# Issuing a 64-column matmul as two of 32 columns in the second half of a sparse graph layer

## The chip, the cores and the metric

The kernel runs on one core of a Trainium2 chip. The metric is the device time of one execution in microseconds. TensorE (PE in the profile) multiplies, with its weight loads counted apart (PEld); VectorE is DVE, ScalarE is ACT, GpSimd is POOL and SyncE is SP.

## What is computed

A graph layer over 4096 nodes, with eight batches of 256 features, all in float32. `x` has the shape (8, 4096, 256), `adj` (4096, 4096), `W` (256, 256).

```python
HW     = einsum('bnf,fo->bno', x, W)
A_norm = relu((adj + adj.T) * 0.5)
D      = sum(A_norm, axis=1)
d      = where(D > 0, where(D > 0, D, 1.0) ** -0.5, 0.0)
L      = eye(N) - d[:, None] * A_norm * d[None, :]
out    = relu(einsum('nm,bmo->bno', L, HW))
y      = layernorm(x + out)
```

The adjacency is sparse and falls off with the node number: the early nodes (hubs) have many neighbours, the late ones few.

## The kernel before

**First phase (to about 595 us).** The adjacency is read in blocks of 512 by 512, transposed on TensorE, added to its mirror, clipped and written to a DRAM tensor `a_dram`. Beside it the products of `x` and `W` are formed, scaled by the inverse root of the degree and written to `g_dram` (4096 rows of 2048 values: eight batches of 256). The block of output rows 0 (tile `lead`) is accumulated here as well.

**Second phase.** The other 31 blocks of 128 output rows are taken two at a time, as 16 units `u`, in the order of `SEQ`: 1 to 7, then 0, then 8 to 15. For a unit the kernel does not multiply by the whole adjacency. It packs the source nodes that have an edge to the unit into tiles of 128 nodes. Nodes are sorted by a kind, a number of four bits that says which of the four half blocks (two blocks, `b` = 0 and 1, with a lower and an upper half of 64 rows each) need them. `CAPS` fixes how many tiles of each kind a unit has; the lists of nodes are worked out on the chip, some units ahead (`patterns`, `place`, `place_rest`, `spread`, `collect`, `index`; their small bf16 matmuls are the lines L226 to L356).

For each tile GpSimd issues two indirect DMAs in `gather`: `ga`, the 128 rows of adjacency (L814, stationary operand), and `g`, the 128 rows of `g_dram` (L827, moving operand, 1 MB, in a ring of `RING` = 12 buffers). A further tile, `g_hub`, holds the first 128 nodes and stays in SBUF for the units in `HUB`.

The products are at L1032. An accumulator `py` of one block is four PSUM banks of 128 x 512 float32, one for each chunk `c` of the 2048 columns. Where a tile serves all 128 rows of a block, the product has 128 stationary columns. Where it serves one half block, it has 64 and writes partitions 0 to 63 or 64 to 127 of the bank. `steps_of` pairs tiles so that a lower and an upper half stand side by side in a step (kinds 1 with 2, 4 with 8, 5 with 10; kinds 6 and 9 hold both halves themselves), and the loop turns a step round where it would begin with the half in which the last one ended:

```python
if work[0][1] == side != slice(0, P):
    work.reverse()
```

Within a step the products of one chunk `c` follow each other, first over the entries of `work` and then over the chunks. Every issue on an engine is chained behind the one before it on that engine (`queue`), so the program's order is the code's order. When a block has had all its products, `finish` evicts its four banks on ScalarE (`evict`, L683), adds the residual and normalises on VectorE, and writes the result by a DMA of SyncE. `lists` puts the list work of later units between the steps of TensorE.

Of the kernel before, what the change touches and what calls it, by code (L numbers as in the profile page):

```python
# [59 lines left out]
def kernel(  # L60
# [25 lines left out]
    nc = tc.nc  # L86
    B, N, F = x.shape
    FO = w.shape[1]
    P = 128
    S = 512  # L90
# [6 lines left out]
    Q = 64  # L97
# [77 lines left out]
    def blocks(u):  # L175

        return min(2, NB - 1 - 2 * u)
# [561 lines left out]
    def targets(u, kind):  # L739

        if kind == 0:
            kind = 15 if blocks(u) == 2 else 3
        out = []
        for b in range(2):
            h = kind >> 2 * b & 3
            if h:
                out.append((b, {1: slice(0, Q), 2: slice(Q, P), 3: slice(0, P)}[h]))
        return out
# [19 lines left out]
    with (  # L768
# [23 lines left out]
        def queue(engine):  # L792

            traced = reversed(nc.cur_bb.bb.instructions)
            return tc.issue_after(next(i for i in traced if i.engine == engines[engine]))

        def gather(n):

            if n >= len(order):
                return  # L800
            u, kind, t = order[n]
            both = len(targets(u, kind)) == 2
            at = apool.tile([P, 2 * P], F32, tag="a", name=f"ga_{u}_{t % tmax}")
            if t < 0:
                if not hub_loads:
                    with queue("pool"):
                        hub_loads.append(nc.gpsimd.dma_start(hub, g_dram[:P, :]))
                with queue("pool"):
                    nc.gpsimd.dma_start(at, a_dram[:P, (2 * u + 1) * P : (2 * u + 3) * P])
                got[u, t] = (at, hub)  # L810
                return
            gi, ai = plan[u]
            with queue("pool"):
                nc.gpsimd.indirect_dma_start(  # L814
                    out=at if both else at[:, :P],
                    out_offset=None,
                    in_=a_pairs if both else a_rows,
                    in_offset=bass.IndirectOffsetOnAxis(ap=ai[:, t : t + 1], axis=0),
                    element_offset=P if both else 0,
                )  # L820


            n = len(ring_tiles)
            gt = ring[n % RING]
            ring_tiles.append(gt)
            with queue("pool"):
                nc.gpsimd.indirect_dma_start(  # L827
                    out=gt,
                    out_offset=None,
                    in_=g_dram,  # L830
                    in_offset=bass.IndirectOffsetOnAxis(ap=gi[:, t : t + 1], axis=0),
                    bounds_check=N if n < RING else N - 1,
                    oob_is_err=False,
                )
            got[u, t] = (at, gt)
# [4 lines left out]
        def after(n, fn, *args):  # L840
            later.append((n, fn, args))

        def run_later(by):
            ready = [l for l in later if l[0] <= by]
            later[:] = [(n - by, fn, args) for n, fn, args in later if n > by]
            for _, fn, args in ready:
                fn(*args)


        u = SEQ[0]  # L850
# [4 lines left out]
        py = {0: lead}  # L855
        left = {}
# [50 lines left out]
        def finish(i):  # L907

            if i == NB - 1:
                finish_last(i)  # L910
                return
            with queue("act"):
                y = evict(i, py.pop(i), ypool)

            def rest():
                z = xr.pop(i)
                with queue("dve"):
                    mv, var = moments(i, y, z, stat)
                with queue("dve"):
                    rstd = inverse_root(i, var, stat)  # L920

                def end():
                    in_turn(normalise, i, z, mv, rstd)

                after(3, end)

            after(1, rest)
# [66 lines left out]
        for q, (u, step) in enumerate(steps):  # L994
            new = q == 0 or steps[q - 1][0] != u
            last = q + 1 == len(steps) or steps[q + 1][0] != u
            if new:
                after(6, prepare, u)
                if q > 0:
                    after(10 if u != SEQ[-1] else 4, residuals, range(2 * u + 1, 2 * u + 1 + blocks(u)))  # L1000
                left = {}
                for v, st in steps[q:]:
                    if v == u:
                        for k, t in st:
                            for b, _ in targets(u, k):
                                left[b] = left.get(b, 0) + 1
                begun = set()
                for b in range(blocks(u)):
                    py[2 * u + 1 + b] = []
            work = [(b, rows, *got[u, t]) for m in range(2) for k, t in step for b, rows in targets(u, k)[m : m + 1]]  # L1010
            if work[0][1] == side != slice(0, P):
                work.reverse()
            side = work[-1][1]
            for b in sorted({wk[0] for wk in work}):
                if not py[2 * u + 1 + b]:
                    py[2 * u + 1 + b] = [
                        psum.tile([P, S], F32, tag=f"b{b}", name=f"py_{u}_{b}_{c}") for c in range(G // S)
                    ]
            fresh = []
            for b, rows, at, gt in work:  # L1020
                hs = {(b, h) for h in range(2) if rows.start <= h * Q < rows.stop}
                assert not hs & begun or hs <= begun
                fresh.append(not hs & begun)
                begun |= hs
                left[b] -= 1
            for c in range(G // S):
                for (b, rows, at, gt), new_rows in zip(work, fresh):
                    both = any(len(targets(u, k)) == 2 for k, t in step)
                    off = b * P if both else 0

                    with queue("pe"):
                        nc.tensor.matmul(  # L1032
                            py[2 * u + 1 + b][c][rows, :],
                            lhsT=at[:, off + rows.start : off + rows.stop],
                            rhs=gt[:, c * S : (c + 1) * S],
                            start=new_rows,
                            stop=left[b] == 0,
                            skip_group_check=True,
                        )
            for k, t in step:  # L1040
                gather(n)
                n += 1
            run_later(sum(1 + (rows == slice(0, P)) for _, rows, _, _ in work))
            for b in {wk[0] for wk in work}:
                if left[b] == 0:
                    finish(2 * u + 1 + b)
                    if b == 0:
                        after(2, lists, u)
# [9 lines left out]
    with tc.If(short > 0):  # L1058
        with (
# [4 lines left out]
            for i in range(NB):  # L1064
# [4 lines left out]
                py = [psum.tile([P, S], F32, tag="b0", name=f"pz_{i}_{c}") for c in range(G // S)]  # L1069
                for m in range(NB):  # L1070
                    gt = full.tile([P, G], F32, tag="g", name=f"gf_{i}_{m}", bufs=4)
                    nc.sync.dma_start(gt, g_dram[m * P : (m + 1) * P, :])
                    for c in range(G // S):
                        nc.tensor.matmul(
                            py[c],
                            lhsT=lt[:, m, :],
                            rhs=gt[:, c * S : (c + 1) * S],
                            start=(m == 0),
                            stop=(m == NB - 1),
# [33 lines left out]
```

## Time and profile before

| what | value |
|---|---|
| three runs | 1523.82, 1530.25, 1533.23 us (median 1530.25) |
| profiled execution | span 1527.5 us; a time of its own beside the span is not recorded |
| TensorE | 1441.2 us busy, 94% of the span, 6440 matmuls |
| weight loads | 763.6 us, 50% |
| VectorE | 983.6 us, 64% |
| GpSimd | 682.0 us, 45% |
| DMA | 564.50 MB, mean 370 GB/s |
| L1032, 64 columns | 2152 records, 494.7 us busy |
| L1032, 128 columns | 720 records with `g`, 176 with `g_hub`: 322.0 and 77.3 us busy |

The span is the time from the first to the last instruction of one execution. A row of a group reads: line, engine, operation, output and inputs, stationary shape, moving shape, count, then the busy time in us and the mean of one in ns, then the engine's idle time before it and what ended that. Busy time of a group counts overlapping records once, so busy time over count is the price of one where several run side by side, and the mean is how long one of them lasts. A row of the timeline reads: start and length in us, engine, line, operation, count. Ends of matmuls are modelled.

### The profile page before, as it was taken

What the parts mean: (1) busy time and instruction counts of PE and PEld (TensorE: products, weight loads), DVE (VectorE), ACT (ScalarE), POOL (GpSimd) and SP (SyncE); (2) the same over time, 40 slices, a digit from 0 to 9 for tenths busy, and PEclk for the clock granted to TensorE, in tenths of its full rate; (3) what the DMA queues carried; (4) which work ended last, traced back from release to release, by engine and by line L of the source; (5) the groups of instructions that cost most, each with busy time, mean ns of one, the idle gap of its engine ahead of it and who ended that gap; (6) DMA issues with size and microseconds to landing.
All of it is one profiled execution on the core that took longest, in us unless ns stands there. A gap on an engine that the chain in (4) does not pass through costs nothing.

```text
span 1527.5 us, 19332 instructions
## 1 busy us (share of the span) xinstructions
PE 1441.2 (94%) x6440; PEld 763.6 (50%) x6440; DVE 983.6 (64%) x3015; ACT 369.0 (24%) x462; POOL 682.0 (45%) x1051
## 2 busy tenths in 40 slices
PE   5999999989989989999999999999999999999995
PEld 5778777767767754433343343333433433333331
DVE  4676578888646463055568769569137688898534
ACT  3655554535434450010100100100010010001111
POOL 3002010010303316666667666666556676656653
PEclk9999999989999999999999999999999999999998
DMA  9999999999879898999999999999979999999995
GB/s 340 365 366 401 393 379 365 359 369 354 344 248 367 332 390 354 401 395 418 361 393 372 402 409 365 393 403 389 384 278 406 346 394 403 405 393 366 379 405 195
DMA packets 216714, 564.50 MB, mean 370 GB/s; under 512 B 16550, under 2 KB 104918, under 8 KB 180134
## 3 DMA queue, kind: packets, MB, share of 16 engines
q0 software_dynamic: 54224, 304.94, 50.4%
q1 hardware_dynamic: 93472, 126.89, 23.8%
q10 hardware_dynamic: 68912, 131.37, 22.7%
q8 instruction: 54, 0.88, 0.2%
q14 instruction: 52, 0.43, 0.1%
HBM read 443.61 MB, written 136.34 MB: 380 GB/s over the span
## 4 chain that ended last, share of the span: by engine, by line
PE 68%; DMA 14%; DVE 9%; issue 5%; POOL 2%; ACT 2%; ACTq 0%; DVEq 0%; POOLq 0%
PE py L1032 49%; PE pg L532 8%; DMA g<-g_dram,gi 6%; PE lead L490 5%; DMA a_dram<-sym 5%; DVE sym L427 3%; PE xtr L521 2%; PE tr L423 2%; DVE part L432 2%; DMA xin<-in_x_dram 2%; DMA ga<-a_dram,ai 1%; ACT sym L431 1%; PE lists L356 1%; ACT xt L522 1%; POOL g L827 0%
## 5 line engine op out<-in xcount | busy, mean ns | idle before, releaser
L1032 PE MATMUL py<-g,ga 128*64 128x512 f32 (+1 forms) x2872 | 813.0, 600 | 18.4 <-DMA g<-g_dram,gi 8.0
L1032 PEld LDWEIGHTS py<-g,ga 128*64 128x64 f32 (+1 forms) x2872 | 293.1, 151 | 525.1 <-issue 493.1
L827 POOL DMA_INDIRECT g<-g_dram,gi x268 | 294.9, 1101 | 219.1 <-PE py L1032 79.1
L814 POOL DMA_INDIRECT ga<-a_dram,ai x268 | 292.0, 1090 | 109.5 <-issue 76.8
L683 ACT ACTIVATE y<-py,minus_r 128x512 f32<-128x512 f32 x120 | 79.9, 687 | 812.3 <-PE py L1032 659.8
L693 DVE TENSOR_TENSOR xr<-xr,y 128x2048 f32<-128x2048 f32 x31 | 71.1, 2294 | 269.1 <-ACT y L683 267.2
L532 PE MATMUL pg<-w_sb,xt 128*128 128x256 f32 x1024 | 232.0, 385 | 5.2 <-ACT xt L522 5.2
L427 DVE TENSOR_TENSOR sym<-tr,adj 128x512 f32<-128x512 f32 x256 | 162.7, 683 | 96.9 <-PE tr L423 80.2
L532 PEld LDWEIGHTS pg<-w_sb,xt 128*128 128x128 f32 x1024 | 195.6, 194 | 33.4 <-ACT xt L522 5.6
L432 DVE TENSOR_REDUCE part<-sym 128x32 f32<-128x2048 f32 x64 | 145.5, 2279 | 62.0 <-ACT sym L431 62.0
L423 PE MATMUL tr<-ident,adj 128*128 128x128 f32 x1024 | 138.4, 285 | 30.6 <-DVE sym L427 19.2
L431 ACT ACTIVATE sym<-sym 128x2048 f32<-128x2048 f32 x64 | 122.6, 1916 | 129.9 <-DVE sym L427 117.5
L452 POOL TENSOR_TENSOR r<-e,neg_half 128x4 f32<-128x4 f32 x8 | 8.3, 1039 | 317.9 <-DVE e L451 236.5
L423 PEld LDWEIGHTS tr<-ident,adj 128*128 128x128 f32 x1024 | 118.6, 146 | 60.4 <-DVE sym L427 32.1
L521 PE MATMUL xtr<-ident,xin 128*128 128x128 f32 x512 | 72.4, 288 | 18.0 <-DVE sym L427 16.5
L702 DVE BATCH_NORM_STATS2 stats<-xr 128x6 f32<-128x256 f32 x256 | 87.0, 413 | 1.1
L726 DVE TENSOR_SCALAR xr<-xr,mv,root 128x256 f32<-128x256 f32 x248 | 83.6, 409 | 0.1
L490 PE MATMUL lead<-gt,strip 128*128 128x512 f32 x176 | 83.0, 598 | 0.0
L522 ACT COPY xt<-xtr 128x512 f32<-128x512 f32 x128 | 68.1, 591 | 46.7 <-PE xtr L521 46.0
L542 ACT ACTIVATE gt<-pg,r 128x512 f32<-128x512 f32 x88 | 60.6, 688 | 74.8 <-PE pg L532 72.3
L1032 PE MATMUL py<-g_hub,ga 128*128 128x512 f32 x176 | 77.3, 592 | 0.0
L521 PEld LDWEIGHTS xtr<-ident,xin 128*128 128x128 f32 x512 | 59.0, 146 | 34.9 <-DVE sym L427 26.4
(142 smaller groups left out, 825.8 us busy)
## 6 DMA issues: line engine op xcount, KB each, us to landing
adj<-in_adj_dram SPq DMA_DIRECT2D x64, 1024.0 KB
a_dram<-sym ACTq DMA_DIRECT2D x64, 1024.0 KB
out_dram<-xr SPq DMA_DIRECT2D x31, 1024.0 KB
xr<-in_x_dram ACTq DMA_DIRECT2D x29, 1024.0 KB
xin<-in_x_dram SPq DMA_DIRECT2D x44, 512.0 KB
g_dram<-gt ACTq DMA_DIRECT2D x22, 1024.0 KB
xin<-in_x_dram POOLq DMA_DIRECT2D x20, 512.0 KB
g_dram<-held ACTq DMA_DIRECT2D x10, 1024.0 KB
```

Of the source, the lines that this page charges most:

```text
L423: ins = nc.tensor.transpose(pt[:, c * P : (c + 1) * P], tji[:, c, a * P : (a + 1) * P], ident)
L427: nc.vector.tensor_add(sym[:, a, :], pt, tij[:, a, :])
L431: nc.scalar.activation(sym, sym, AF.Relu, scale=0.5)
L432: nc.vector.tensor_reduce(part[:, i * A : (i + 1) * A, j * S // Q : (j + 1) * S // Q], sym.rearrange("p a (c q) -> p a c q", q=Q), AX.X, A ...
L490: nc.tensor.matmul(lead[c], lhsT=strip, rhs=g[:, c * S : (c + 1) * S], start=not done, stop=len(done) == NB - 1, skip_group_check=True,)
L521: nc.tensor.transpose(pt[:, k, c, :], xin[b // H][:, b % H + k, c * P : (c + 1) * P], ident)
L532: ins = nc.tensor.matmul(pg[:, k * FO : (k + 1) * FO], lhsT=xt[:, b + k, c, :], rhs=w_sb[:, c, :], start=(c == 0), stop=(c == FC - 1),)
L702: nc.vector.bn_stats(stats[:, b, :], z[:, b, :])
L726: nc.vector.tensor_scalar(z[:, b, :], z[:, b, :], mv[:, b, 0:1], rstd[:, b : b + 1], ALU.subtract, ALU.mult,)
L814: nc.gpsimd.indirect_dma_start(out=at if both else at[:, :P], out_offset=None, in_=a_pairs if both else a_rows, in_offset=bass.IndirectOff ...
L827: nc.gpsimd.indirect_dma_start(out=gt, out_offset=None, in_=g_dram, in_offset=bass.IndirectOffsetOnAxis(ap=gi[:, t : t + 1], axis=0), boun ...
L1032: nc.tensor.matmul(py[2 * u + 1 + b][c][rows, :], lhsT=at[:, off + rows.start : off + rows.stop], rhs=gt[:, c * S : (c + 1) * S], start=ne ...
```

## The change

In units 8 to 15 a product with 64 stationary columns is issued as two products with 32 columns, over the same moving operand and into the same bank, each to its own 32 partitions. With a lower and an upper half in turn, successive products stand in the column places 0, 1, 2 and 3 of the array. Products of 128 columns, and all of units 0 to 7, stay as they are. The number of multiplications, the bytes moved and the order of the tiles do not change; the number of matmuls and weight loads does.

```diff
-                    with queue("pe"):
-                        nc.tensor.matmul(
-                            py[2 * u + 1 + b][c][rows, :],
-                            lhsT=at[:, off + rows.start : off + rows.stop],
-                            rhs=gt[:, c * S : (c + 1) * S],
-                            start=new_rows,
-                            stop=left[b] == 0,
-                            skip_group_check=True,
-                        )
+                    n_rows = rows.stop - rows.start
+                    by = P // 4 if n_rows == Q and u >= 8 else n_rows
+                    for lo in range(rows.start, rows.stop, by):
+                        with queue("pe"):
+                            nc.tensor.matmul(
+                                py[2 * u + 1 + b][c][lo : lo + by, :],
+                                lhsT=at[:, off + lo : off + lo + by],
+                                rhs=gt[:, c * S : (c + 1) * S],
+                                start=new_rows,
+                                stop=left[b] == 0,
+                                skip_group_check=True,
+                            )
```

## The prediction

> **What bounds the kernel now.** I read the page first (shares of the engines, slices over the span), then the chain of waits for the stretch of the units that change, then the groups by line with shapes kept apart, and last the weight loads in order of time. On the page:
>
> ```profile
> PE 1441.2 (94%) x6440; PEld 763.6 (50%) x6440; DVE 983.6 (64%) x3015; ACT 369.0 (24%) x462; POOL 682.0 (45%) x1051
> ...
> PE   5999999989989989999999999999999999999995
> ...
> DMA  9999999999879898999999999999979999999995
> ```
>
> TensorE (PE) is busy in nearly every slice, and so are the DMA engines: two resources stand close together. By counting the records of L1032 along the order that the program writes out, unit 8 begins at 1145.4 us and unit 15 ends at 1514.4 us, so the changed units fill 369.0 us. The chain of waits cut to that stretch says:
>
> ```profile
> by line: PE py L1032 62.9%; DMA g<-g_dram,gi 22.2%; DMA ga<-a_dram,ai 5.3%; issue 5.0%; POOL g L827 1.7%; POOL ga L814 0.8%; PE lists L356 0.7%; DVE xr L876 0.3%; DVE incl_k L184 0.2%; ACT y L866 0.2%; DVE pos_k L188 0.1%; PE lists L226 0.1
> ```
>
> The product sets the end for 62.9% of the stretch; the gathers of g and ga for 27.5% (the late units 13 to 15). So time added to L1032 goes to the end almost whole; time taken off it would soon meet the gathers. The groups over the whole span, shapes apart:
>
> ```profile
> L1032 PE MATMUL py<-g,ga 128*64 128x512 f32 x2152 | 494.7, 601 | 14.9 <-DMA g<-g_dram,gi 8.0 <-issue 3.8 <-DVE pos_k L188 2.2
> L1032 PE MATMUL py<-g,ga 128*128 128x512 f32 x720 | 322.0, 597 | 3.5 <-issue 3.0
> ...
> L1032 PEld LDWEIGHTS py<-g,ga 128*64 128x64 f32 x2152 | 159.4, 138 | 336.5 <-issue 314.8 <-DMA ga<-a_dram,ai 7.9 <-DMA g<-g_dram,gi 4.8
> L1032 PEld LDWEIGHTS py<-g,ga 128*128 128x128 f32 x720 | 133.7, 190 | 188.7 <-issue 178.3 <-DMA ga<-a_dram,ai 7.8 <-DMA g<-g_dram,gi 1.6
> ```
>
> Two things are to be seen. First, the counts: the code issues 1524 products in this loop, and the page has 2872 + 176 = 3048 records, so each float32 product is two records (a load and a matmul each, called a and b below). Second, one record of 128 columns takes 322.0/720 = 0.447 us of PE, one of 64 columns 494.7/2152 = 0.230 us, though each lasts about 600 ns alone. Two records of 64 columns therefore run side by side for the price of one wide one: half the array is not idle now. The loads in order of time, around the last step of unit 1 (a lone product in the lower half, four times) and the start of unit 2:
>
> ```profile
> 673.85 0.14 PEld L1032 LDWEIGHTS py<-g,ga 128*64 128x64 f32 x1 [0.29 <-issue]
> 674.28 0.14 PEld L1032 LDWEIGHTS py<-g,ga 128*64 128x64 f32 x1 [0.29 <-issue]
> 674.71 0.19 PEld L1032 LDWEIGHTS py<-g,ga 128*64 128x64 f32 x3 [0.29 <-issue]
> 675.14 0.14 PEld L1032 LDWEIGHTS py<-g,ga 128*64 128x64 f32 x1 [0.23 <-issue]
> ...
> 802.01 0.14 PEld L1032 LDWEIGHTS py<-g,ga 128*64 128x64 f32 x2 [0.28 <-issue]
> 802.44 0.14 PEld L1032 LDWEIGHTS py<-g,ga 128*64 128x64 f32 x2 [0.29 <-issue]
> 802.87 0.14 PEld L1032 LDWEIGHTS py<-g,ga 128*64 128x64 f32 x2 [0.29 <-issue]
> ```
>
> In the steady state (the last three lines) two loads come every 0.43 us; call 0.429 us a slot. In the first four lines one place works alone, one load a slot, and at 674.71 the other place joins while the lone product still has three records to run. It starts ahead of records that stand before it in the program.
>
> **What the Trainium skill says.** (1) "TensorEngine Tiling (Array Packing)", Key Properties: tiles load and multiply independently, and a change of tiling mode drains the array. The trace agrees for two columns (0.230 against 0.447 us), and from one form to the other the starts stand 0.522 us apart where 0.429 is usual, so a drain costs 0.093 us. (2) "TensorE: Matmul & The Clock Gate", Measured speedup vs the span model: three column tiles of 32 gave 2.38x, sixteen tiles of 32 by 32 gave 10.6x. No run here shows 32 columns, so this is my only support for four at once. (3) The same page, What overlaps and what doesn't: matmuls keep strict program order. The lines at 674.71 disagree, and I follow the trace. (4) "FP8 and Floating Point Precision", TensorE Precision Notes: true float32 takes four passes. That fits two records a product, each of 429 ns.
>
> **The change part by part.**
>
> *Slots.* Units 8 to 15 hold 114 half-width products for each of the four column chunks, 456 in all, hence 912 records of 64 columns. At two a slot they take 456 slots: 456 x 0.429 = 195.6 us. After the change there are 1824 records of 32 columns. At four a slot they take 1824/4 = 456 slots, again 195.6 us. A matmul streams the same 512 elements however few columns are loaded, so narrow ones pay only by standing side by side. Steps in which one half stands alone (in units 8 and 14) do not gain: their two pieces fill two of four places, in as many slots as now.
>
> *Order.* The program writes a and b of one place before the next place. In strict order only two neighbours could overlap. The trace showed a record starting past three pending ones; a piece of the fourth place must pass the b records of the other three, just that many. So four at once needs no more than has been seen, but no margin is shown.
>
> *Weight loads.* 912 more. From 138 ns at 64 columns and 190 at 128 I estimate 112 ns at 32 (0.81 ns a column). Each place needs one a slot, and loads of different places now run together (two in 0.14 us above), so 0.429 us covers them. Were they serial, four would take 0.45 us a slot: 456 x 0.02 = 9 us.
>
> *Issue.* 32 small products of the lists take 0.80 us in the chain (line L356), 25 ns for a load and a matmul. Four pairs need 0.10 us of a 0.429 us slot: hidden.
>
> *Changes of form.* The 64-column records of these units lie in 15 stretches between wide or bf16 work, and they stay 15, so their drains remain. If the fourth place trails by one slot, each stretch ends up to 0.43 us later: 0 to 6.4 us, and I take 0.5, since the order seen needs no trailing. New is the border from unit 0 (64 columns) to unit 8 (32): the upper half now starts three slots early beside the lone product there (at 1144.56, as at 674.71); behind a drain that is lost: 3 x 0.429 + 0.1 = 1.4 us.
>
> *What is untouched.* The gathers, the evictions (they wait for the last piece of a bank, up to 21 ns later at 7 ns a start), the bytes and every other engine's order. The ring of 12 is given back at the same slot.
>
> Sum: 0 + 0 + 0.5 + 1.4, about +2 us, with bounds 0 and +17 (6.4 + 9 + 1.4). A gain below nothing is excluded in the steady state because a slot is set by streaming; only jitter of gathers could give one. Against the profiled execution (span 1527.5 us; its own run among the three is not marked) this is 1529.5. The median of the runs, 1530.25, lies 2.75 above the span, so the same +2 gives about 1532.
>
> **The rivals.**
>
> *A, four at once (forecast):* 1532, own range 1524 to 1544.
>
> *B, partly side by side.* Four streams of float32 from SBUF, or four open places, are more than the trace has shown. With three places on average: 1824/3 = 608 slots, 152 more, 65 us. Waits for gathers inside the stretches give some back: the last stretches last 30.1, 14.0 and 13.4 us where slots ask 20.6, 10.3 and 12.0, so some 15 us can hide it. +50 us: 1580. For it: 64 columns show no sign of how many streams fit. Against it: two streams run without a nanosecond lost (429 in both forms).
>
> *C, two at once; this is the case on the other side.* If the array lets only two matmuls overlap, or keeps a and b in order so that only neighbours meet, each group of eight records takes four slots and not two: 912 slots, +195.6 us, less the 15: about 1711. For it: point (3), strict order. Against it: 674.71 and 1144.56. It decides as soon as a slot of four lasts over 0.429 + (15.3 + 15)/456 = 0.495 us, which is where the time leaves 1%.
>
> *D, faster.* Shorter loads in front of 15 stretches save 15 x 0.03 us; more could come only from gathers that happen to land better: 1526 at best likely.
>
> A change that does nothing would show 128*64 in units 8 to 15; the slices in the diff leave no room for that.
>
> **How the numbers follow.** A 0.59, B 0.17, C 0.20, D 0.04. A measurement of this kernel tells about 1% from no change. A lies within 1%; D mostly does too, with 0.02 beyond; B and C are slower, and I leave 0.03 of A's tail there. Hence faster 0.02, same 0.60, slower 0.38. The time is A's, 1532. To hold eight in ten the range takes in A, D and most of B, up to 1640, and leaves out C.
>
> **What would show it.** Right: a group 128*32 of 1824 records with 0.11 to 0.12 us of PE each, four loads together every 0.43 us, unit 8 to 15 in about 371 us, and the gathers still 20% to 30% of the chain there. Wrong: 0.15 us or more a record (B) or 0.21 to 0.23 (C), loads two by two at 0.43 us, gathers gone from the chain, and the waits of POOL for PE grown.

## The result

The change took 1548.41 us against 1528.66 for the kernel before (medians of 4 each): ratio 1.0135, 95% interval 1.0114 to 1.0157. It is slower by about 20 us. The forecast was 1532, within 1% of no change; the measured time lies inside the range given and outside the forecast's own case (1524 to 1544).

The profiled execution spans 1543.6 us, 16.1 more than the one before. Lines of its page, the slices and the group that is new, with its loads:

```profile
PE 1461.4 (95%) x7352; PEld 779.0 (50%) x7352; DVE 983.3 (64%) x3015; ACT 369.5 (24%) x462; POOL 691.4 (45%) x1051
...
PE   5999989898979989999999999999999999999996
...
DMA  9999999999879998999999999999989999999995
```

```profile
L1035 PE MATMUL py<-g,ga 128*32 128x512 f32 x1824 | 226.5, 593 | 9.0 <-issue 7.1
...
L1035 PEld LDWEIGHTS py<-g,ga 128*32 128x32 f32 x1824 | 79.2, 110 | 149.8 <-issue 145.6
```

The 1824 records of 32 columns are there, and one costs 226.5/1824 = 0.124 us of PE. Two at a time would be 0.21. So four do run side by side, nearly always; the price at four without a gap is 0.429/4 = 0.107. The idle time before them is ended by "issue", not by a gather: TensorE waited for nothing that the profile shows. The chain of waits, cut from the start of unit 8 to the end of unit 15, says the same:

```profile
by line: PE py L1035 95.8%; issue 2.3%; PE lists L356 1.2%; DVE xr L876 0.3%; PE lists L226 0.2%; ACT y L866 0.2%; PE lists L227 0.2%; PE lists L303 0.0%; PE lists L302 0.0%
```

The gathers, 27.5% of this stretch before, are gone from it: TensorE became later than they are.

Where the time went is seen when the narrow records are cut into stretches between wide or bf16 work. A middle stretch (kinds 6, 9, 5 and 10) follows wide products. An edge stretch (kinds 4 and 8, then 1 and 2 of the next unit) follows the list products. Lengths in us, from the start of the first record to the start of what comes next; "slots" is the count of slots by 0.429:

| stretch | slots | before | change | change, other session (`change3` below) |
|---|---|---|---|---|
| middle of unit 9 | 13.73 | 13.88 | 13.87 | 13.87 |
| edge 8 to 9 | 13.73 | 13.88 | 19.82 | 13.87 |
| edge 9 to 10 | 13.73 | 14.35 | 19.87 | 13.87 |
| edge 10 to 11 | 13.73 | 13.88 | 19.81 | 13.87 |
| edge 11 to 12 | 10.30 | 14.54 | 15.11 | 14.38 |
| edge 12 to 13 | 13.73 | 13.88 | 17.02 | 13.87 |
| edge 13 to 14 | 12.01 | 13.88 | 17.57 | 13.87 |
| edge 14 to 15, no lists | 20.59 | 30.63 | 22.99 | 30.55 |

The seven edge rows come to 115.0 us before and 132.2 with the change, 17.2 more; the short stretch at the start of unit 8 adds 2.4. That makes 19.6 us, the loss of the medians. (In these two profiles the units ahead of unit 8 ended 2.7 us earlier with the change, so the spans differ by less.) The edge stretches alone would cost more, but the last one gives 7.6 us back: before, TensorE waited there for gathers, and a later TensorE does not. The loads in order of time, in the stretch from unit 9 to 10:

```profile
1258.15 0.11 PEld L1035 LDWEIGHTS py<-g,ga 128*32 128x32 f32 x1 [0.17 <-issue]
1258.58 0.19 PEld L1035 LDWEIGHTS py<-g,ga 128*32 128x32 f32 x2 [0.32 <-issue]
1259.39 0.11 PEld L1035 LDWEIGHTS py<-g,ga 128*32 128x32 f32 x1 [0.62 <-issue]
1260.79 0.14 PEld L1035 LDWEIGHTS py<-g,ga 128*32 128x32 f32 x2 [1.29 <-issue]
1262.21 0.14 PEld L1035 LDWEIGHTS py<-g,ga 128*32 128x32 f32 x2 [1.29 <-issue]
1263.64 0.24 PEld L1035 LDWEIGHTS py<-g,ga 128*32 128x32 f32 x8 [1.29 <-issue]
```

For 5 us only one or two loads come every 0.7 or 1.4 us, and at 1263.64 eight at once; such a place is called a thin spot below. The waits in front of these loads are all ended by "issue", none by a transfer. In the stretches at 13.87 us, four loads come every 0.43 us. The clock is not the reason: the mean granted clock is 0.984 in this profile and 0.981 in the one before.

### The profile page after: what moved, and what is told of

Same layout as the page of the kernel before. It is cut to its first block, busy times and chain, and to the rows that moved or that the text cites. A ratio compares the mean times of both kernels' runs of the same rounds, so it can differ in the third digit from the quotient of the medians.

```text
span 1543.6 us, 21156 instructions
## 1 busy us (share of the span) xinstructions
PE 1461.4 (95%) x7352; PEld 779.0 (50%) x7352; DVE 983.3 (64%) x3015; ACT 369.5 (24%) x462; POOL 691.4 (45%) x1051
## 4 chain that ended last, share of the span: by engine, by line
PE 74%; DMA 9%; DVE 8%; issue 5%; ACT 2%; POOL 2%; ACTq 0%; DVEq 0%; POOLq 0%
PE py L1035 54%; PE pg L532 9%; PE lead L490 5%; DMA g<-g_dram,gi 4%; DMA a_dram<-sym 3%; PE tr L423 3%; DVE sym L427 3%; PE xtr L521 3%; DVE part L432 2%; DMA xin<-in_x_dram 2%; ACT sym L431 1%; PE lists L356 1%; POOL limit L165 0%; POOL base L166 0%; ACT xt L522 0%
## 5 line engine op out<-in xcount | busy, mean ns | idle before, releaser
L1035 PE MATMUL py<-g,ga 128*32 128x512 f32 (+2 forms) x3784 | 831.3, 595 | 16.1 <-issue 12.4
L1035 PEld LDWEIGHTS py<-g,ga 128*32 128x32 f32 (+2 forms) x3784 | 307.2, 134 | 527.2 <-issue 507.0
L827 POOL DMA_INDIRECT g<-g_dram,gi x268 | 306.9, 1145 | 238.2 <-PE py L1035 116.5
L814 POOL DMA_INDIRECT ga<-a_dram,ai x268 | 288.4, 1076 | 94.2 <-issue 81.1
L335 DVE TENSOR_TENSOR hot<-iota_q,at 128x1024 bf16<-128x1024 f32 x64 | 74.7, 1227 | 2.8 <-DMA a_dram<-sym 2.8
```

The costliest lines, as they stand in the source:

```text
L814: nc.gpsimd.indirect_dma_start(out=at if both else at[:, :P], out_offset=None, in_=a_pairs if both else a_rows, in_offset=bass.IndirectOff ...
L827: nc.gpsimd.indirect_dma_start(out=gt, out_offset=None, in_=g_dram, in_offset=bass.IndirectOffsetOnAxis(ap=gi[:, t : t + 1], axis=0), boun ...
L1035: nc.tensor.matmul(py[2 * u + 1 + b][c][lo : lo + by, :], lhsT=at[:, off + lo : off + lo + by], rhs=gt[:, c * S : (c + 1) * S], start=new_ ...
```

## The experiments

A session below is one set of runs on one chip, with the kernel before beside it. Two explanations stood at first. Theory I: TensorE runs out of issued instructions, because each slot now needs twice as many. Theory P: the four places, or the form of 32 columns, cost something.

**Twice the instructions without the 32 columns (`n256`).** From the kernel before, in the steps of units 8 to 15 that hold half-width products only:

```diff
-            for c in range(G // S):
+            half = u >= 8 and all(rows != slice(0, P) for _, rows, _, _ in work)
+            width = S // 2 if half else S
+            for c in range(G // width):
+                lo = c * width % S
...
-                            rhs=gt[:, c * S : (c + 1) * S],
-                            start=new_rows,
+                            rhs=gt[:, c * width : (c + 1) * width],
+                            start=new_rows and lo == 0,
```

> Before, with the half-width products of units 8 to 15 split along the moving operand instead: 64 columns stay, and each product of 512 moving elements becomes two of 256. The number of loads and matmuls in these units is that of the change (1824 records), but two column places are used and a record streams half as long, so the array needs the same 195.6 us. Theory I (TensorE runs out of issued instructions: the count is what costs): slower than before by 15 to 25 us, ratio 1.010 to 1.016, with records arriving one by one in the stretches that follow the list products. Theory P (four places or the 32-column form cost something themselves): no change, ratio 0.998 to 1.003.

Measured: 1553.72 against 1528.16 us, ratio 1.0159 (1.0129 to 1.0188). The groups:

```profile
L1035 PE MATMUL py<-g,ga 128*64 128x256 f32 x1824 | 221.2, 387 | 18.4 <-issue 16.3 <-DMA ga<-a_dram,ai 1.2
```

The same 1824 records, two places, no 32 columns, and the same loss with the same "issue" before it. Where the slots ask 13.73 us, its middle stretches last 13.96 and its edge stretches 19.3 to 21.6. Theory P falls: what the two programs share is the number of instructions.

**One kind of stretch at a time (`mid`, `edge`).**

```diff
-                    by = P // 4 if n_rows == Q and u >= 8 else n_rows
+                    by = P // 4 if n_rows == Q and u >= 8 and not {k for k, _ in step} & {1, 2, 4, 8} else n_rows
```

for `mid`, and the same without `not` for `edge`.

> The change only in the steps of kinds 5, 6, 9 and 10, that is in the stretches that follow wide products. Theory I: these stretches start with a full queue and lost nothing in the profile after, so no change against before, ratio 0.998 to 1.003. Theory P: about 4/9 of the loss (8 of 18 us), ratio about 1.005 to 1.006.

> The change only in the steps of kinds 1, 2, 4 and 8, the stretches that begin right after the list products. Theory I: the whole loss of the change, +15 to +22 us, ratio 1.010 to 1.015. Theory P: 5/9 of it, about +10 us, ratio about 1.007.

Measured: `mid` 1528.42 us, ratio 1.0006 (0.9984 to 1.0028); `edge` 1549.51 us, ratio 1.0146 (1.0121 to 1.0171). Within these intervals all of the loss belongs to the edge stretches.

**VectorE's short instructions moved away (`late`).** Each edge stretch of 19.8 us holds two thin spots, and VectorE runs short instructions of some 0.17 us in both: mostly those of the normalisation (L705 to L721) in the first, its list work in the second. Only the list work was moved.

```diff
-            after(6, read, True)
+            after(10, read, True)
...
-                after(6, prepare, u)
+                after(10, prepare, u)
```

> The change with the second part of VectorE's list work (read, last) put off from 6 to 10 steps' counts and the spread behind it (prepare, 6 to 10), so that VectorE's run of short instructions falls beside wide products. Theory D (the short instructions of VectorE hold up TensorE's issue): the second of the two thin spots in each edge stretch (some 5 us long, 3 us lost) goes, ratio against before about 1.006. Theory B (the burst of list products on TensorE itself empties the queue): nothing changes, ratio 1.012 to 1.015.

Measured: 1546.96 us, ratio 1.0134 (1.0104 to 1.0164). The edge stretches from unit 8 to 11 lasted 15.65, 19.88 and 19.08 us: the second thin spot went in the first of them only. In the next, from unit 9 to 10, it stood where it had been while VectorE ran no list work:

```profile
1258.22 0.14 PEld L1035 LDWEIGHTS py<-g,ga 128*32 128x32 f32 x2 [1.08 <-issue]
1259.66 0.12 PEld L1035 LDWEIGHTS py<-g,ga 128*32 128x32 f32 x2 [1.29 <-issue]
```

```profile
1258.96 2.29 DVE L693 TENSOR_TENSOR xr<-xr,y 128x2048 f32<-128x2048 f32 x1 [1.96 <-issue]
1261.29 2.71 DVE L702 BATCH_NORM_STATS2 stats<-xr 128x6 f32<-128x256 f32 x8
```

The second thin spot does not need that list work, so theory D falls as the cause of the loss. It is not shown that the list work has no part (the stretch from unit 8 to 9 lost its second spot), and the short instructions in the first spot were not moved. Theory B, the burst of list products, was left.

**Gathers held back, and a burst of its own (`hold`, `burst`).**

```diff
-            for k, t in step:
-                gather(n)
-                n += 1
+            debt += len(step)
+            edge = {9: {4, 8}, 10: {1, 2}, 11: {4, 8}, 12: {1, 2}}.get(u, set())
+            if not edge & {k for k, _ in step}:
+                for _ in range(min(debt, len(step) + 2)):
+                    gather(n)
+                    n += 1
+                    debt -= 1
```

```diff
+            if q >= 2 and u == 15 and steps[q - 1][0] == 15 and steps[q - 2][0] != 15:
+                burst = psum.tile([P, S], F32, tag="b1", name="burst")
+                for _ in range(36):
+                    with queue("pe"):
+                        nc.tensor.matmul(burst[:, :28], lhsT=ones, rhs=ones[:, :28], start=True, stop=True)
```

> The change with the gathers that GpSimd would issue in two of the edge stretches (last steps of unit 9 with first steps of unit 10, and units 11 with 12) held back into the steps after them; the list products there stay. The other edge stretches are the control in the same run. Theory G (GpSimd's issue of gathers, back to back in these stretches only, slows TensorE's supply of instructions): the stretches from unit 9 to 10 and 11 to 12 last 13.9 and 10.5 us, the others stay at 17 to 20. Theory B (the burst of list products): all stay 5 to 6 us over their slots. The time of the whole says little, since the DMA engines stand still for some microseconds and must make up for it.

> The change with 36 small bf16 products into a free bank added after the second step of unit 15, where no gathers are issued any more and no lists are made. Its last stretch ran at full rate in the change (192 records, four a slot, the last 2.4 us over being waits). Theory B: TensorE's records thin out 2 us after the burst for some 3 us. Theory G: they go on at four a slot.

Measured: one time each, 1526.42 and 1530.58 us, against 1524.29 for before on that chip. Neither expectation was met. No edge stretch of either, the untouched ones included, shows the loss: the rows from 8 to 9, 9 to 10 and 10 to 11 all lasted 13.87 us, and the later ones up to unit 14, where gathers are waited for, lasted about as long as before (14.38 us from unit 11 to 12 in `hold`). In `burst` nothing ahead of unit 15 differs from the change, which had lost 6 us in each of those. So the thin spots do not seem to follow from the code alone, and these two runs decide nothing between theory G (the gathers of GpSimd) and theory B.

**The same programs again (`again`, `burst2`, `n256b`, then `change3`).** Nothing edited.

> The change itself once more. The two kernels before this one (gathers held back in two places; a burst in unit 15) ran all their edge stretches at four a slot, also where they do not differ from the change. Theory R (whether TensorE's instructions come fast enough depends on the chip or the placement of a run, not on the code): if this run is on a chip like theirs, the change costs nothing here, ratio 0.998 to 1.003, edge stretches 13.9 us. Theory C (something in those two programs removed the thin spots): the change costs 1.2% to 1.5% wherever it runs, edge stretches 17 to 20 us.

> The kernel with 36 small products after the second step of unit 15, unchanged from its first run. Theory R: it stands with the change in the same call, both with thin edge stretches or both without, ratio within 0.004 of it. Theory C: no thin stretches, ratio about 1.003, whatever the change shows.

> The kernel with 64 columns and the moving operand split into two of 256, unchanged from its first run (ratio 1.0159 there). Theory R: with the change in the same call: no loss where the change shows none, 1.3% to 1.8% where it shows one. Theory C: 1.3% to 1.8%.

Measured in one session: the change 1548.33 us, ratio 1.0134 (1.0110 to 1.0158); `burst2` 1550.05, 1.0133 (1.0111 to 1.0155); `n256b` 1546.81, 1.0109 (1.0079 to 1.0138). The program that had run through at full rate now had the thin edge stretches (19.80, 19.84 and 19.78 us). That is theory R: the same code with and without the loss. The low end of what was expected of `n256b` was 1.3%; it lost 1.1%.

These runs have the loss, so `burst2` also answers what `burst` was made to ask. Its added burst and the loads behind it:

```profile
1524.81 0.97 PEld L1050 LDWEIGHTS <-ones 128*128 128x128 bf16 x36 [0.84 <-issue]
1525.80 0.16 PEld L1035 LDWEIGHTS py<-g,ga 128*32 128x32 f32 x8
...
1527.97 0.13 PEld L1035 LDWEIGHTS py<-g,ga 128*32 128x32 f32 x4 [0.30 <-issue]
1528.40 0.13 PEld L1035 LDWEIGHTS py<-g,ga 128*32 128x32 f32 x4 [0.30 <-issue]
```

All 64 records behind the burst took 7.00 us, where slots ask 6.86. Theory B expected them to thin out after 2 us for some 3 us; theory G expected four a slot. VectorE ran the short instructions of the normalisation meanwhile (1525.16 to 1527.8 us), while GpSimd issued no gathers. In this one place, then, a burst and those short instructions together made no thin spot. A shorter thin spot of the same run (loads at 1515.56, 1516.29 and 1517.01 us) comes 56 us after its last list product, while gathers had been issued up to 1515.98 us.

The gathers also fit in time. Behind the second thin spot that was shown for the change, loads resume in full at 1263.64 us, 1.34 us after the end of the last gather before a pause of GpSimd:

```profile
1261.35 0.95 POOL L814 DMA_INDIRECT ga<-a_dram,ai  x1 [0.30 <-issue]
1264.12 1.01 POOL L827 DMA_INDIRECT g<-g_dram,gi  x1 [1.82 <-remote]
```

In the three stretches from unit 8 to 11 all six thin spots of the change end in this way, 0.75 to 1.35 us after the end of such a gather. That is no proof: GpSimd also pauses because it waits for TensorE to give a buffer back, and `hold`, which would have parted the two, was not run in a session with the loss. Theory G is favoured, not shown.

Such a session can be told by VectorE alone. Its short instructions at L261, in the groups cut to 620 to 1500 us, first in the change, then in the kernel before (the profile that the prediction was read from), then in the last session:

```profile
L261 DVE TENSOR_TENSOR upto<-ends,off 128x2 f32<-128x2 f32 (+1 forms) x84 | 11.9, 158 | 12.4 <-DVE off L260 7.2 <-DVE more L277 2.9 <-DVE upto L261 1.5
```

```profile
L261 DVE TENSOR_TENSOR upto<-ends,off 128x2 f32<-128x2 f32 (+1 forms) x84 | 12.1, 160 | 8.0 <-DVE off L260 3.2 <-DVE upto L261 1.6 <-DVE more L277 1.4
```

```profile
L261 DVE TENSOR_TENSOR upto<-ends,off 128x2 f32<-128x2 f32 (+1 forms) x84 | 11.9, 160 | 0.8
```

The same 84 instructions, each as long, with 12.4, 8.0 and 0.8 us of waiting in front of them. The mean distance between the short instructions of lines 246 to 299 was 225 to 242 ns in every trace of the sessions with thin stretches, in the profile of before as well, and 180 to 181 ns in the three traces without (`hold`, `burst`, `all64`). That was put to the test last:

> The change itself, a third time, on whatever chip comes. Theory R (the supply of instructions differs from chip to chip): VectorE's list work tells which kind of chip it is, by the mean distance of its short instructions (180 ns in the three traces without thin stretches, 230 ns in those with them); at 180 ns the change is within 0.3% of before and its edge stretches last 13.9 us, at 230 ns it loses 1.1% to 1.6% and they last 17 to 20 us. A chip of 180 ns with a loss, or one of 230 ns without, ends theory R.

Measured: 1523.51 us against 1523.34, ratio 0.9999 (0.9985 to 1.0014), with a distance of 180 ns. Its groups and its loads in an edge stretch:

```profile
L1035 PE MATMUL py<-g,ga 128*32 128x512 f32 x1824 | 208.3, 601 | 7.6 <-DMA g<-g_dram,gi 5.6 <-DVE pos_k L188 2.0
```

```profile
1251.20 0.13 PEld L1035 LDWEIGHTS py<-g,ga 128*32 128x32 f32 x4 [0.30 <-issue]
1251.63 0.13 PEld L1035 LDWEIGHTS py<-g,ga 128*32 128x32 f32 x4 [0.30 <-issue]
1252.06 0.13 PEld L1035 LDWEIGHTS py<-g,ga 128*32 128x32 f32 x4 [0.30 <-issue]
```

208.3 us is what the 914 records of 64 columns took in the same units before (208.3, in the groups cut to that stretch). Four loads every 0.43 us, the idle time ended by gathers, and the total unchanged: here the forecast holds. The gathers are 22.6% of the chain from 1142.3 to 1508 us, inside the 20% to 30% that was forecast.

The kernel before differs between the sessions too: its median is 1528.16 to 1528.99 us in the three with the loss and 1524.29 and 1523.34 in the two without. So a ratio means something only within one session.

**No change of form (`all64`, `all64b`).** If places are free and drains are not, wide products could be issued as two of 64.

```diff
-                    with queue("pe"):
-                        nc.tensor.matmul(
-                            py[2 * u + 1 + b][c][rows, :],
-                            lhsT=at[:, off + rows.start : off + rows.stop],
+                    for lo in range(rows.start, rows.stop, Q):
+                        with queue("pe"):
+                            nc.tensor.matmul(
+                                py[2 * u + 1 + b][c][lo : lo + Q, :],
+                                lhsT=at[:, off + lo : off + lo + Q],
```

> The kernel before with every product of 128 columns in this loop issued as two of 64, in all units, so that the array does not change its form between steps. There are some 55 changes between 64 and 128 columns, each run between them 0.16 to 0.2 us over its slots: some -9 us, ratio 0.994, if the supply of instructions holds at four records a pair of slots; +5 us or more if the doubled count of the wide steps lets the queue run out in the edge stretches (theory I reaching to 64 columns).

> Wide products as two of 64 in all units, unchanged (ratio 0.9992 on a chip of 180 ns). On a chip of 230 ns: the wide steps now ask for twice the instructions and leave a less full queue, so +3 to +10 us, ratio 1.002 to 1.007. On one of 180 ns: 0.998 to 1.001 as there.

Measured: 1523.58 against 1524.29 us, ratio 0.9992 (0.9980 to 1.0004), and 1521.39 against 1523.34, ratio 0.9985 (0.9968 to 1.0002), both at 180 ns. Not faster beyond the interval, so the 0.994 expected was not reached, and not tried where the supply is thin. The waits in front of these products grew instead:

```profile
L1033 PE MATMUL py<-g,ga 128*64 128x512 f32 x3592 | 806.0, 597 | 23.2 <-DMA g<-g_dram,gi 21.0 <-DVE pos_k L188 2.0
```

21.0 us of waiting for g, where the profile of before had 8.0 and `change3`, without the loss too, 11.8 in its three groups of products with g. This fits a TensorE that comes earlier and meets the gathers; how much the drains gave back was not measured apart.

## Why the prediction was right or wrong

**Slots: right.** Four records share a slot in every middle stretch that has the 32 columns (13.87 us for 13.73), and in the full edge stretches of the sessions with a quick supply. Rivals B and C, three or two at once, did not happen: a record of 32 columns cost 0.123 to 0.127 us in the sessions with the loss (0.141 in `edge`, which has them only where the thin spots are) and 0.114 in `change3`, against 0.143 for three and 0.21 for two. The measured total of 1548 was nearer to a weak form of B in time, but not by its mechanism. That it lies inside the range is therefore luck: the range went that far up for B, and the forecast's own case ended at 1544.

**Order: right.** Four a slot without a lost slot is what a record of the fourth place gives when it passes the b records of the other three.

**Weight loads: right.** 110 ns against 112 estimated, four in 0.13 us.

**Changes of form: right in size.** Middle stretches exceed their slots by 0.14 us, before by 0.15. The start of unit 8 lasted 7.0 us in the quick session where 6.2 were left to it before, the lost lead of the upper half and a drain: +0.8 against 1.4.

**Issue: this is the step that failed.** "Four pairs need 0.10 us of a 0.429 us slot: hidden." The 25 ns came from the list products, and those are a short burst. They show how fast TensorE took instructions for 0.80 us, not how fast they follow over a stretch of 14 us. In the session of the result the supply fell short in two spots of most edge stretches. Before, with four instructions a slot (two loads, two matmuls), the full edge stretches of such a session lasted 13.88 to 14.35 us; with eight they lasted 17.0 to 19.9. Priced at nothing, the term measured 20 us there and nothing in the quick sessions. Two signs that were named for B and C, gathers gone from the chain and longer waits of GpSimd for TensorE (79.1 us before L827, then 116.5), came true for this reason. The cover, too, was misnamed: the slot hides the issue only while the supply keeps up.

**What the profile of before could have told.** The 8.0 us in front of L261 are VectorE standing idle, put down to work of its own; in the quick session they are 0.8. I read only the lines of TensorE, and a slow supply was showing on the engine beside it. Without the 0.8 to compare, the 8.0 could have raised the question, not answered it.

**Chances.** I gave 0.38 to slower, nearly all of it for the array (B and C). The parts named add up to 0.40 (0.17 + 0.20 + 0.03 of A's tail), and same to 0.58; the slip changes nothing. The mean slot of the change, 4 x 0.124 = 0.497 us, lies near the 0.495 at which 1% was to be lost, but that is chance: by the same division the kernel before had 208.3/456 = 0.457 us a slot, not 0.429, so the change added 0.040 us a slot, 18 us.

**Still open.** Why the supply differs between sessions. It is not the program, and two sessions with opposite behaviour carry the same chip number. The larger of the two queues that the page calls instruction moved 61 packets and 1.00 MB in the change and in `change3` alike, so the amount does not tell them apart. Every time on record has a span and a granted clock beside it, so each execution seems to have been recorded, and no run tells whether the recording takes part. Why the supply falls short in the edge stretches and not in the middle ones is open too: a burst of small products is not enough (`burst2`), VectorE's list work is not needed for the second thin spot (`late`), and the gathers, back to back there, were never held back in a session with the loss.

## What to carry to other kernels

Splitting a matmul over more column places cost the array nothing here and gained nothing, since the places were already full; what it spends is instructions. Price issue by a stretch that holds the rate for long, not by a burst, and look whether other engines with short instructions show waits that nothing in the profile explains. A loss of 1% from issue can be there in one session and gone in the next, so repeat such a comparison in more than one before you believe its sign.

## What was not expected of the hardware

- Column places run ahead of each other past three pending records, and four float32 streams of 512 elements share a slot of 429 ns without loss for 17 us on end (160 records in 17.30 us).
- Behind a burst of 36 small products, in the same session as thin spots elsewhere, 64 records of 32 columns kept four a slot (7.00 us for 6.86), with no gathers being issued.
- The same program lost 1.3% or nothing by session. In a thin spot instructions come at steps of about 0.71 us or twice that, and VectorE stepped with TensorE: loads at 1262.21 and 1263.64 us, VectorE's held-up instructions at 1262.23 and 1263.66:

```profile
1262.23 0.16 DVE L261 TENSOR_TENSOR upto<-ends,off 128x2 f32<-128x2 f32 x1 [0.55 <-DVE more L277]
...
1263.66 0.16 DVE L260 TENSOR_TENSOR off<-free,upto 128x2 f32<-128x2 f32 x1 [0.47 <-DVE off L260]
```

That two engines resume together points to something that they share in being supplied; it was not tested further.
